# Four fused transformer blocks on one core: batches regrouped from threads of 2, 2, 2, 2 into threads of 1, 2, 2, 2, 1, with other early work and another order of loads

## The chip, the cores and the metric

The kernel runs on one core of a Trainium2 chip, in one launch. The metric is the device time of that launch in microseconds, the lower the better. A core has a matrix engine (PE in the profile, with its weight loads as PEld), a vector engine (DVE), a scalar engine (ACT), a general engine (POOL, GpSimd) and a queue engine (SP) that here only issues DMA transfers. [...]

## The reference

Eight batches of 128 tokens with 256 features (`x`), and a context of the same shape, go through four blocks one after the other, all in float32. The token count and width never change, so what one batch does is independent of the other batches.

```
x = L0(x, ctx)            # attention on ctx, 16 heads of 16 (a0); MLP 256->1024->256 (m0)
x = L1(ctx, x, mask)      # attention on ctx and x together (a1); MLP (m1)
x = L2(x, ctx, ctx)       # two wide attentions on ctx, 16 heads of 128 (l1, l2),
                          # each with a learned extra key and value; MLP (m2)
x = L3(x, ctx, masks)     # self-attention (a4), attention on ctx (a5); MLP (m3)

def _cross_attention(q_in, kv_in, ...):             # the wide attention of L2
    kh = concatenate([(kv_in @ wk + bk), bias_k])   # 16 heads of 128
    vh = concatenate([(kv_in @ wv + bv), bias_v])
    weights = softmax(qh @ kh.T / sqrt(128))
    return (weights @ vh) @ wo + bo
```

Each block adds its result to `x` behind layer norms. The weights are the same for all batches.

## The kernel before, in words

**Threads.** The eight batches are cut into four "threads" of two batches by `SIZES = (2, 2, 2, 2)` (line 25). A thread takes its batches through a0, m0, a1, m1 (its front), then the wide attentions l1 and l2 in four head groups each (its wide part), then m2, a4, a5 and m3 (its back); this is `blocks` (line 1351). A thread loads every weight for itself, with a `loader` (line 505) that holds at most `NW` = 4 of the thread's weight tiles and shares `NWT` = 11 with the others. So each thread moves the full set of weights and bias rows, whatever number of batches it has. Thread h above 1 starts when the front of thread h-2 is done, and above 2 also needs the wide part of thread h-3 to be done.

**The order is planned when the program is built.** The threads are Python generators. A planner (`Plan`, line 83) steps through them with its own estimate of every instruction's duration (`_weight`, line 263) and of the matrix engine's clock (`Clock`, line 226). Whenever an engine is free in that plan, it writes out the most urgent instruction that is ready. The result is a fixed order for each engine. Urgency is a number for each kind of work (`U`, line 64) plus one for each stage of each thread (`LATE`, line 65). When the plan sees the matrix engine idle[...], `idle_work` (line 393) puts in a 128x128 product of the identity matrix whose result nobody reads. I call these fillers; the profile shows them as `mm<-ident`.

**Projections.** `proj` (line 534) multiplies weights, as the stationary operand of 128x128, with the transposed activations of the whole thread: two batches are 256 moving columns. Values, the way back and the scores are made batch by batch, so their shapes do not depend on the thread's size. The front's attentions run one item for each batch (a0) or two (a1), at most two in flight (`flight`, line 445).

**Early wide work.** `AHEAD` (line 63) names head groups whose wide keys and values are computed before the thread's own front, since they need only the context: thread 0 does those of groups 0 and 1 of l1.

**Loads.** All transfers are issued by SP, through `load` and `dma` (lines 408 to 415), in the plan's order, mostly with urgency 0. `value_bias` (line 1282) loads two rows for each wide head group, `bv` and `bb`, spread over 128 partitions, and POOL subtracts them. `bb` has a single buffer; in this version the program takes no slot for it, so the second load of `bb` is issued to SP at once and waits there for the buffer. `inputs` (line 1404) loads `x`, the bias columns `cols` and the context of each thread, and starts it.

Of the kernel before, what the change touches and what calls it, by code (L numbers as in the profile page):

```python
# [15 lines left out]
ALU = mybir.AluOpType  # L16
# [5 lines left out]
NC = D // P  # L22
FF = 4 * D
NF = FF // P
SIZES = (2, 2, 2, 2)
NW, NWT = 4, 11
BIG = 1.0e30

# [31 lines left out]


WARM = True
AHEAD = [[(1, 0), (1, 1)], [], [], []]
U = {'take': 0.33, 'taken': -1, 'norm': 0.36, 'mask': 1.35, 'k': 2.41, 'q': 1.92, 'v': 2.5, 'by key': 0.5, 'softmax': 2.4, 'weights': 0.74, 'pairs': 0.3, 'out': 0.94, 'mlp norm': 0.75, 'mlp 1': 3.6, 'mlp 2': 2.28, 'wide norm': -1, 'wide k': 3.49, 'wide q': 4.0, 'wide v': 4.5, 'wide s': 1.19, 'wide': -0.42, 'ahead': 2.48}
LATE = [(2.3, -0.18, 0.84, -0.88, 1.83, -0.17, 2.53, 1.2, 3.66, 1.59), (7.76, 6.61, 5.49, 5.66, 1.7, 0.2, 4.52, 3.1, 7.31, 7.88), (1.86, 2.79, 2.79, -0.1, 2.14, -1, 4.58, 4.78, 5.62, 1.93), (0.03, 1.63, -0.02, 0.92, 0.05, 2.99, -1, 0.16, -1, -1)]


class Event:
# [14 lines left out]
class Plan:  # L83
# [28 lines left out]
    def spawn(self, gen, urgency, after=0):  # L112
        end = Event()
        self.live[id(gen)] = gen
        self._later(self.now + after, (gen, urgency, end), None)
        return end
# [68 lines left out]
        return start + self.weight  # L185

    def run(self):
        self.now = max(self.until.values())
        while self.events or self.asked:
            while self.events and self.events[0][0] <= self.now:  # L190
                _, _, proc, value = heapq.heappop(self.events)
                self._step(proc, value)
            for eng in self.until:
                if self.until[eng] <= self.now:
                    got = self._choose(eng)
                    if not got and eng == "PE" and self.idle_work and (self.events or self.asked):
                        self.weight = 0
                        if self.clock.lazy(self.now) and self.idle_work():
                            self.until[eng] = self._end(eng)
                            self.log.append((eng, self.now, self.until[eng] - self.now, "idle", 2))  # L200
                    if got:
                        _, a, (_, ns, f, lat, table), load = got
                        self.asked.remove(a)
                        self.weight, self.shared, self.wrote, self.count = ns, False, [], 0
                        if load:
                            self.weight += 1295
                            self.table = table[0]
                        value = f()
                        end = self._end(eng)
                        self.until[eng] = end  # L210
                        self.log.append((eng, self.now, end - self.now, f.__qualname__.replace("four_blocks.<locals>.", "").replace("<locals>.", ""), self.count))
                        self._later(end + (self.SEEN[eng] if lat is None else lat), a[2], value)
            at = [self.events[0][0]] if self.events else []
            at += [t for t in self.until.values() if t > self.now]
            if not at:
                break
            self.now = max(self.now, min(at))
        stuck = []
        for g in self.live.values():
            while g:  # L220
                stuck.append(f"{g.gi_code.co_name}:{g.gi_frame.f_lineno}")
                g = g.gi_yieldfrom
        assert not stuck, f"waits without end: {stuck}"


class Clock:


    W, LITTLE, MUCH = 3413, 0.48, 0.87

    def __init__(self):
        self.t, self.busy, self.fast = 0.0, 0.0, False
# [3 lines left out]
    def lazy(self, now):  # L236

        self._go(now, False)
        self.spans = [(a, b) for a, b in self.spans if b > now - self.W]
        return not self.fast or sum(b - max(a, now - self.W) for a, b in self.spans) < 0.55 * self.W  # L240

    def _go(self, to, busy):
        while self.t < to:
# [19 lines left out]
def _weight(eng, name, args, kw):  # L263

    aps = [x for x in (*args, *kw.values()) if isinstance(x, bass.AP)]
    sizes = [x.free_size() for x in aps]
    n = max(sizes)
    by_part = sum(m == 1 for m in sizes[1:]) if n > 2 else max(0, len(aps) - 2) if name == "tensor_scalar" else 0
    on_sbuf = all(x.space == bass.MemoryType.SB for x in aps)
    if eng == "PE":  # L270
# [9 lines left out]
    if eng == "ACT":  # L280
        if "accum_out" in kw:
            return 385, False
        if name == "copy":
            return 61 + 0.824 * n, False
        return 127 + 0.805 * n + (40 if isinstance(kw.get("bias"), bass.AP) else 0) + (
            90 if isinstance(kw.get("scale"), bass.AP) else 0), False
    if eng == "DVE":
        if name == "reciprocal":
            return 65 + 6.25 * n, False
        if name in ("bn_stats", "bn_aggr"):  # L290
            return (325 if name == "bn_stats" else 99), False
# [47 lines left out]


def op(eng, f, lat=None, table=None):
    return ((eng, 60 if eng == "SP" else 0, f, lat, table),)


EXP = ("exp",)
# [5 lines left out]
def four_blocks(ctx: ExitStack, tc: tile.TileContext, a: dict, out: bass.AP):  # L351
# [36 lines left out]
    row_slots, bv_slots, w_slots = Slots(2), Slots(2), Slots(NWT)  # L388

    def kb():  # L390
        return new(act, [P, 2 * P], "kb", bufs=20)
# [22 lines left out]
    def load(dst, src, kb_):  # L414
        return dma(lambda: nc.sync.dma_start(out=dst, in_=src), kb_)

    ident = new(const, [P, P], "ident")
    make_identity(tc.nc, ident)
# [86 lines left out]
    def loader(T):  # L505
        names = list(weight_list())
        first = {f"l{i}{hg}{x}" for i, hg in AHEAD[T.h] for x in "kv"}
        ahead = [x for x in names if x[0] in first]
        names = [x for x in names if x[0] not in first]
        for name, shape, pieces in names[:2] + ahead + names[2:]:  # L510
            yield (T.w_slots, 1)
            yield (w_slots, 1)
            t = T.w[name] = new(wpool, shape, "w", bufs=NWT)
            ends = [spawn(load(at(t), src, int(np.prod(shape)) // 256 // len(pieces)), 0) for at, src in pieces]
            T.w_in.setdefault(name, Event())
            spawn(all_then(ends, T.w_in[name]), 0)

# [32 lines left out]
    def asks(r):  # L550
        yield r
# [613 lines left out]
    def keys_values(T, i, hg, step_back):  # L1165

        n = f"l{i}{hg}"
        ks, vs = [], []
        bv = new(wpool, [P, 512], "bv", bufs=2)
        bv_in = spawn(value_bias(bv, i, hg), U["mask"] + step_back)  # L1170
        nb, nt = T.nb, T.nt
        v_in = [Event() for _ in range(nb)]

# [22 lines left out]
        def values():  # L1196
# [3 lines left out]
            for b in range(nb):  # L1200
# [9 lines left out]
                        )  # L1210

                def take(p, b=b, t=t):
                    yield op("DVE", lambda: nc.vector.tensor_tensor(t, p, bv, ALU.add))
                    plan.set(v_in[b])
                yield from product([f], take)
            drop(T)
# [74 lines left out]
    def after_scores(T, i, hg, b, s, vs, v_in, n):  # L1291
        t = new(act, [P, 516], "t", bufs=NT_).rearrange("p (h k) -> p h k", h=4)
# [111 lines left out]
    def inputs():  # L1404
        for T in threads:
            h = T.h
            if h == 0:
                first = new(const, [P, 1], "first")
                spawn(asks(op("ACT", lambda: nc.scalar.activation(first, ident[:, :1], AF.Exp), None, EXP)), 0)
            e = spawn(load(T.x, a["x"][T.batches].rearrange("b p d -> p b d"), 128 * T.nb), 0)  # L1410
            spawn(all_then([e], T.ready), 0)
            if h == 0:
                e = spawn(load(cols, a["cols"], 140), 0)
                spawn(all_then([e], cols_in), 0)
            e = spawn(load(T.ctx, a["ctxT"].rearrange("(c p) t -> p c t", p=P)[:, :, T.tokens], 128 * T.nb), 0)
            spawn(all_then([e], ctx_in[h]), 0)
# [48 lines left out]
```

## Time and profile before

| | |
|---|---|
| median of 3 runs | 1214.67 us (1213.44 to 1214.82) |
| the profiled execution | 1218.14 us, of which its span is 1216.3 us |
| mean granted clock of the matrix engine | 0.986 |
| busy: PE, DVE, ACT, POOL | 1163.1, 747.2, 560.3, 340.2 us |
| fillers on PE | 26.5 us in 128 instructions |
| moved by DMA | 145.59 MB, mean 120 GB/s |

Nearly every instruction goes through one helper, so the profile puts it at line 329; groups are told apart by the tiles that they write and read. `mm`, `tl` and `sc` are PSUM tiles: `mm` holds projections and MLP products, `tl` transposes and wide attention products, `sc` the scores of the small attentions. `mm<-hT,w` is a product of normed activations with a weight, `mm<-ctxT,w` one of the context with a weight; `tl<-kb,kb` are the wide scores. One float32 product of full depth stands as two matrix instructions in the trace. The busy time of PE counts a filler as busy[...], so busy is not the same as useful.

### The profile page before, as it was taken

What the parts mean: (1) busy time and instruction counts of PE and PEld (TensorE: products, weight loads), DVE (VectorE), ACT (ScalarE), POOL (GpSimd) and SP (SyncE); (2) the same over time, 40 slices, a digit from 0 to 9 for tenths busy, and PEclk for the clock granted to TensorE, in tenths of its full rate; (3) what the DMA queues carried; (4) which work ended last, traced back from release to release, by engine and by line L of the source; (5) the groups of instructions that cost most, each with busy time, mean ns of one, the idle gap of its engine ahead of it and who ended that gap; (6) DMA issues with size and microseconds to landing.
All of it is one profiled execution on the core that took longest, in us unless ns stands there. A gap on an engine that the chain in (4) does not pass through costs nothing.

```text
span 1216.3 us, 21992 instructions
## 1 busy us (share of the span) xinstructions
PE 1163.1 (96%) x8352; PEld 950.5 (78%) x8352; DVE 747.2 (61%) x1927; ACT 560.3 (46%) x1428; POOL 340.2 (28%) x393
## 2 busy tenths in 40 slices
PE   7998999999999999999999999999999999998988
PEld 6686778888787788887778887887878888876767
DVE  4665846764666384784776725554545475868872
ACT  3345344453443243457365423332424363686962
POOL 3011201122112032044243201121221272566870
PEclk9899998999999999999999999999999999999999
DMA  7623232335325534252532455344454535332120
GB/s 224 198 62 122 71 100 50 105 109 156 104 90 176 172 120 139 89 164 65 150 96 84 126 168 164 102 156 139 148 163 135 150 118 157 107 98 84 38 73 18
DMA packets 107321, 145.59 MB, mean 120 GB/s; under 512 B 6736, under 2 KB 66256, under 8 KB 107216
## 3 DMA queue, kind: packets, MB, share of 16 engines
q1 hardware_dynamic: 107216, 144.18, 38.9%
q8 instruction: 66, 1.08, 0.4%
q14 instruction: 39, 0.32, 0.1%
HBM read 143.11 MB, written 1.05 MB: 119 GB/s over the span
## 4 chain that ended last, share of the span: by engine, by line
PE 74%; DVE 16%; ACT 4%; DMA 3%; issue 1%; POOL 1%; SPq 0%; ACTq 0%; POOLq 0%; DVEq 0%
PE mm L329 54%; PE tl L329 15%; PE sc L329 5%; DVE t L329 2%; DVE tm L329 2%; DVE rz L329 1%; DVE mx L329 1%; DVE mp L329 1%; ACT t L329 1%; DVE q L329 1%; ACT q L329 1%; DVE rv L329 1%; DVE sm L329 1%; POOL t L329 1%; DVE st L329 1%
## 5 line engine op out<-in xcount | busy, mean ns | idle before, releaser
L329 PE MATMUL mm<-hT,w 128*128 128x256 f32 x1216 | 285.7, 383 | 5.5 <-ACT hT L329 1.9
L329 PEld LDWEIGHTS mm<-hT,w 128*128 128x128 f32 x1216 | 224.5, 191 | 42.6 <-ACT kb L329 3.6
L329 POOL TENSOR_TENSOR t<-t,sm 128x512 f32<-128x512 f32 x128 | 131.9, 1042 | 342.7 <-DVE sm L329 265.6
L329 PE MATMUL mm<-ctxT,w 128*128 128x256 f32 x608 | 146.2, 386 | 8.0 <-DVE kb L329 3.6
L329 PE MATMUL mm<-w,ctxT 128*128 128x512 f32 (+1 forms) x352 | 144.6, 542 | 3.9 <-ACT q L329 2.9
L329 POOL TENSOR_TENSOR x<-x,row 128x512 f32<-128x512 f32 x40 | 50.8, 1270 | 318.1 <-ACT xn L329 117.2
L329 PEld LDWEIGHTS mm<-ctxT,w 128*128 128x128 f32 x608 | 112.8, 192 | 25.9 <-issue 4.8
L329 DVE TENSOR_TENSOR x<-mm,x 128x256 f32<-128x256 f32 (+1 forms) x96 | 48.7, 508 | 122.3 <-PE mm L329 121.6
L329 PE MATMUL mm<-w,at 128*128 128x256 f32 x512 | 121.2, 381 | 1.1 <-DVE vw L329 1.1
L329 PE MATMUL mm<-w,kb 128*128 128x256 f32 x512 | 116.5, 380 | 0.0
L329 PEld LDWEIGHTS mm<-w,at 128*128 128x128 f32 x512 | 95.0, 190 | 17.6 <-issue 3.2
L329 PEld LDWEIGHTS mm<-w,kb 128*128 128x128 f32 x512 | 95.8, 190 | 14.6 <-issue 1.3
L329 ACT ACTIVATE t<-t,mn 128x128 f32<-128x128 f32 x256 | 99.0, 393 | 6.0 <-DVE mn L329 5.1
L329 PEld LDWEIGHTS mm<-w,ctxT 128*128 128x128 f32 x352 | 64.5, 193 | 43.5 <-issue 33.1
L329 POOL TENSOR_TENSOR t<-t,mask 128x512 f32<-128x512 f32 x64 | 80.0, 1275 | 13.8 <-DVE t L329 10.8
L329 PE MATMUL tl<-ident,t 128*128 128x128 f32 x512 | 75.6, 277 | 6.2 <-POOL t L329 2.1
L329 ACT ACTIVATE kb<-mm,cols 128x256 f32<-128x256 f32 x128 | 53.0, 472 | 58.9 <-PE mm L329 58.6
L329 PEld LDWEIGHTS tl<-ident,t 128*128 128x128 f32 x512 | 60.0, 142 | 24.6 <-issue 8.9
L329 ACT ACTIVATE kb<-mm,sb 128x256 f32<-128x256 f32 x72 | 32.7, 471 | 91.4 <-PE mm L329 90.6
L329 ACT ACTIVATE at<-tl,cols 128x128 f32<-128x128 f32 x188 | 53.4, 369 | 44.2 <-PE tl L329 44.1
L329 ACT ACTIVATE t<-t 128x516 f32<-128x516 f32 x64 | 40.4, 633 | 72.1 <-DVE t L329 71.9
L329 PEld LDWEIGHTS tl<-kb,kb 128*128 128x128 f32 x512 | 64.3, 192 | 10.3 <-issue 7.7
(118 smaller groups left out, 1800.5 us busy)
## 6 DMA issues: line engine op xcount, KB each, us to landing
w<-in_L_wk SPq DMA_DIRECT2D x32, 512.0 KB, 4.0
w<-in_L_wv SPq DMA_DIRECT2D x32, 512.0 KB, 4.2
w<-in_L_wq SPq DMA_DIRECT2D x32, 512.0 KB, 4.0
w<-in_L_wo SPq DMA_DIRECT2D x32, 512.0 KB, 4.0
bv<-in_L_bv SPq DMA_DIRECT2D x32, 256.0 KB, 4.5
bb<-in_L_bias_v SPq DMA_DIRECT2D x32, 256.0 KB, 5.3
w<-in_L_mlp_w SPq DMA_DIRECT2D x16, 512.0 KB, 4.2
w<-in_L_w_fc SPq DMA_DIRECT2D x16, 512.0 KB, 4.0
```

The source lines that it names most:

```text
L329: return f(*args, **kw)
```

## The change

The batches are cut into five threads of 1, 2, 2, 2 and 1. The early keys and values are those of group 0 of l1 in thread 1, where before they were those of groups 0 and 1 in thread 0. Weight and value-bias loads get an urgency of their own (`U["load"]`), so that the plan may put more urgent loads ahead of them. Inputs of the first two threads, `cols` and thread 0's weights of a0 may also be issued by ACT. The single buffer of `bb` gets a slot (`bb_slots`), so that its load is issued only when the buffer is free, and `bv` is made inside `value_bias` when its slot is there. The planner's figures, the urgencies and the clock thresholds are other numbers. What is computed for each batch is the same.

```
-SIZES = (2, 2, 2, 2)
+SIZES = (1, 2, 2, 2, 1)
-AHEAD = [[(1, 0), (1, 1)], [], [], []]
+AHEAD = [[], [(1, 0)], [], [], []]
-U = {'take': 0.33, ...
+U = {'take': -0.38, ... 'load': -0.79}
...
-        self.now = max(self.until.values())
+        self.until.update({"DVE": 1900, "POOL": 1500, "PE": 1500})
...
-    W, LITTLE, MUCH = 3413, 0.48, 0.87
+    W, LITTLE, MUCH = 3413, 0.41, 0.84
...
-        return not self.fast or sum(...) < 0.55 * self.W
+        return not self.fast or sum(...) < 0.52 * self.W
...
-    return ((eng, 60 if eng == "SP" else 0, f, lat, table),)
+    return ((eng, 480 if eng == "SP" else 0, f, lat, table),)
...
-    def dma(f, kb_):
-
-        yield op("SP", f)
+    def dma(f, kb_, early):
+
+        yield op("SP", lambda: f(nc.sync)) + (op("ACT", lambda: f(nc.scalar)) if early else ())
         plan.dma_until = max(plan.dma_until, plan.now) + kb_ * 2.8
-        yield plan.dma_until - plan.now + 1900
+        yield plan.dma_until - plan.now + 2300
...
-            ends = [spawn(load(at(t), src, ...), 0) for at, src in pieces]
+            early = T.h == 0 and name.startswith("a0")
+            ends = [spawn(load(at(t), src, ..., early), U["load"] - 2 * early)
+                    for at, src in pieces]
...
-        bv = new(wpool, [P, 512], "bv", bufs=2)
-        bv_in = spawn(value_bias(bv, i, hg), U["mask"] + step_back)
+        bv = []
+        bv_in = spawn(value_bias(bv, i, hg, step_back), U["mask"] + step_back)
...
-    def value_bias(bv, i, hg):
+    def value_bias(to, i, hg, step_back):
         s = slice(hg * 512, (hg + 1) * 512)
         yield (bv_slots, 1)
+        bv = new(wpool, [P, 512], "bv", bufs=2)
+        to.append(bv)
+        e = spawn(load(bv, a[f"L2_bv{i}"][:, s].partition_broadcast(P), 256), U["load"] + step_back)
+        yield (bb_slots, 1)
         bb = new(wpool, [P, 512], "bb", bufs=1)
-        e = spawn(load(bv, a[f"L2_bv{i}"][:, s].partition_broadcast(P), 256), 0)
-        yield from load(bb, a[f"L2_bias_v{i}"][:, s].partition_broadcast(P), 256)
+        yield spawn(load(bb, a[f"L2_bias_v{i}"][:, s].partition_broadcast(P), 256), U["load"] + step_back)
         yield e
         yield op("POOL", lambda: nc.gpsimd.tensor_tensor(bv, bv, bb, ALU.subtract))
+        plan.put(bb_slots)
...
     def inputs():
         for T in threads:
             h = T.h
+            early = h < 2
+            rows = (load(T.x, ..., 128 * T.nb, early),
+                    load(T.ctx, ..., 128 * T.nb, early))
+            for f, then in zip(rows, (T.ready, ctx_in[h])):
+                spawn(all_then([spawn(f, -3)], then), 0)
             if h == 0:
+                spawn(all_then([spawn(load(cols, a["cols"], 140, True), -3)], cols_in), 0)
...
-            yield 2000 if h == 0 else 8000
+            yield 4000 if h == 0 else 8000
```

The built program of after holds 481 DMA issues on SP and 5 on ACT, where before had 389 on SP. On PE the shapes that change are these (products of full depth, each two matrix instructions):

| product | before | after |
|---|---|---|
| `mm<-hT,w` and `mm<-ctxT,w`, 256 columns | 912 | 684 |
| the same, 128 columns | 0 | 456 |
| fillers | 64 | 36 |

More of the change, by code (lines that the diff above doesn't have):

```diff
@@ L62 @@
 WARM = True
-AHEAD = [[(1, 0), (1, 1)], [], [], []]
-U = {'take': 0.33, 'taken': -1, 'norm': 0.36, 'mask': 1.35, 'k': 2.41, 'q': 1.92, 'v': 2.5, 'by key': 0.5, 'softmax': 2.4, 'weights': 0.74, 'pairs': 0.3, 'out': 0.94, 'mlp norm': 0.75, 'mlp 1': 3.6, 'mlp 2': 2.28, 'wide norm': -1, 'wide k': 3.49, 'wide q': 4.0, 'wide v': 4.5, 'wide s': 1.19, 'wide': -0.42, 'ahead': 2.48}
-LATE = [(2.3, -0.18, 0.84, -0.88, 1.83, -0.17, 2.53, 1.2, 3.66, 1.59), (7.76, 6.61, 5.49, 5.66, 1.7, 0.2, 4.52, 3.1, 7.31, 7.88), (1.86, 2.79, 2.79, -0.1, 2.14, -1, 4.58, 4.78, 5.62, 1.93), (0.03, 1.63, -0.02, 0.92, 0.05, 2.99, -1, 0.16, -1, -1)]
+AHEAD = [[], [(1, 0)], [], [], []]
+U = {'take': -0.38, 'taken': -1, 'norm': 1.14, 'mask': 4.04, 'k': 2.03, 'q': 0.38, 'v': 2.36, 'by key': 0.44, 'softmax': 1.41, 'weights': 0.4, 'pairs': -0.29, 'out': 1.85, 'mlp norm': 0.59, 'mlp 1': 2.92, 'mlp 2': 3.5, 'wide norm': 1.7, 'wide k': 3.4, 'wide q': 3.15, 'wide v': 4.5, 'wide s': 4.05, 'wide': 0.0, 'ahead': 1.27, 'load': -0.79}
+LATE = [(2.57, -1, -0.28, 0.19, 2.33, 0.01, 3.97, 2.35, 3.3, -0.36), (11.45, 1.43, 1.9, 4.16, -1, -0.96, 3.26, 5.22, 7.47, 5.41), (2.13, 8.62, 4.45, 3.2, 2.52, 0.88, 2.33, 2.26, 2.52, 7.8), (5.21, 8.07, 3.05, 0.78, -0.4, 1.37, 2.54, -0.03, -0.89, 2.66), (1.56, -1, -0.88, 1.22, -0.63, 1.37, 5.13, 1.3, 1.03, 1.13)]
 class Event:
@@ L239, in lazy @@
         self.spans = [(a, b) for a, b in self.spans if b > now - self.W]
-        return not self.fast or sum(b - max(a, now - self.W) for a, b in self.spans) < 0.55 * self.W
+        return not self.fast or sum(b - max(a, now - self.W) for a, b in self.spans) < 0.52 * self.W
     def _go(self, to, busy):
@@ L267, in _weight @@
     n = max(sizes)
+    if name == "dma_start":
+        return 480, False
     by_part = sum(m == 1 for m in sizes[1:]) if n > 2 else max(0, len(aps) - 2) if name == "tensor_scalar" else 0
@@ L284, in _weight @@
             return 61 + 0.824 * n, False
-        return 127 + 0.805 * n + (40 if isinstance(kw.get("bias"), bass.AP) else 0) + (
+        return 127 + 0.805 * n + (35 if on_sbuf and n == 256 else 0) + (40 if isinstance(kw.get("bias"), bass.AP) else 0) + (
             90 if isinstance(kw.get("scale"), bass.AP) else 0), False
     if eng == "DVE":
+        if name == "tensor_scalar" and n == 4 and len(aps) == 2 and len(args) > 5:
+            return 145, False
         if name == "reciprocal":
@@ L290, in _weight @@
         if name in ("bn_stats", "bn_aggr"):
-            return (325 if name == "bn_stats" else 99), False
+            return (330 if name == "bn_stats" else 150), False
         if n <= 8:
@@ L387, in four_blocks @@
     attn_lock, x1_slots = Slots(2), Slots(2)
-    row_slots, bv_slots, w_slots = Slots(2), Slots(2), Slots(NWT)
+    row_slots, bv_slots, bb_slots, w_slots = Slots(2), Slots(2), Slots(1), Slots(NWT)
     def kb():
@@ L406, in col, with load @@
         return cols[:, at : at + n]
-    def dma(f, kb_):
-        yield op("SP", f)
+    def dma(f, kb_, early):
+        yield op("SP", lambda: f(nc.sync)) + (op("ACT", lambda: f(nc.scalar)) if early else ())
         plan.dma_until = max(plan.dma_until, plan.now) + kb_ * 2.8
-        yield plan.dma_until - plan.now + 1900
-    def load(dst, src, kb_):
-        return dma(lambda: nc.sync.dma_start(out=dst, in_=src), kb_)
+        yield plan.dma_until - plan.now + 2300
+    def load(dst, src, kb_, early=False):
+        return dma(lambda eng: eng.dma_start(out=dst, in_=src), kb_, early)
     ident = new(const, [P, P], "ident")
@@ L513, in loader @@
             t = T.w[name] = new(wpool, shape, "w", bufs=NWT)
-            ends = [spawn(load(at(t), src, int(np.prod(shape)) // 256 // len(pieces)), 0) for at, src in pieces]
+            early = T.h == 0 and name.startswith("a0")
+            ends = [spawn(load(at(t), src, int(np.prod(shape)) // 256 // len(pieces), early), U["load"] - 2 * early)
+                    for at, src in pieces]
             T.w_in.setdefault(name, Event())
@@ L1212, in take @@
                 def take(p, b=b, t=t):
-                    yield op("DVE", lambda: nc.vector.tensor_tensor(t, p, bv, ALU.add))
+                    yield op("DVE", lambda: nc.vector.tensor_tensor(t, p, bv[0], ALU.add))
                     plan.set(v_in[b])
@@ L1406, in inputs @@
             h = T.h
+            early = h < 2
+            rows = (load(T.x, a["x"][T.batches].rearrange("b p d -> p b d"), 128 * T.nb, early),
+                    load(T.ctx, a["ctxT"].rearrange("(c p) t -> p c t", p=P)[:, :, T.tokens], 128 * T.nb, early))
+            for f, then in zip(rows, (T.ready, ctx_in[h])):
+                spawn(all_then([spawn(f, -3)], then), 0)
             if h == 0:
+                spawn(all_then([spawn(load(cols, a["cols"], 140, True), -3)], cols_in), 0)
                 first = new(const, [P, 1], "first")
[L1409 to L1416, printed above, removed]
+                spawn(asks(op("ACT", lambda: nc.scalar.activation(first, ident[:, :1], AF.Exp), None, EXP)), 9)
             spawn(blocks(T), 0)
-            yield 2000 if h == 0 else 8000
+            yield 4000 if h == 0 else 8000
     plan.idle_work = idle_work if WARM else None
```

## Prediction

> **What bounds the kernel now.** I read the page first (busy times, slices), then the stages by window, then the shapes of PE's instructions, then the head in order of time.
>
> ```profile
> span 1216.3 us, 21992 instructions
> PE 1163.1 (96%) x8352; PEld 950.5 (78%) x8352; DVE 747.2 (61%) x1927; ACT 560.3 (46%) x1428; POOL 340.2 (28%) x393
> PEclk9899998999999999999999999999999999999999
> ...
> 0.00:200.00 200.00, 180.10 (x1592) 142.39 (x1596) 121.17 (x347) 83.64 (x145) 32.72 (x64) 0.93 0.40 123
> 200.00:550.00 350.00, 344.79 (x2435) 284.90 (x2430) 223.19 (x559) 153.22 (x322) 72.88 (x86) 1.00 0.41 125
> 550.00:650.00 100.00, 93.81 (x717) 74.86 (x716) 67.00 (x165) 57.43 (x173) 40.25 (x45) 0.98 0.37 109
> 650.00:1050.00 400.00, 395.02 (x2353) 325.19 (x2352) 221.18 (x557) 151.95 (x377) 94.58 (x105) 1.00 0.45 138
> 1050.00:1216.30 166.30, 149.38 (x1272) 123.15 (x1270) 114.71 (x302) 114.05 (x416) 99.75 (x95) 0.99 0.22 67
> ```
>
> PE is the bound, but "96% busy" hides slack: it counts fillers, and slow instructions at half clock. So I price PE's work at the full-clock rate of dense bursts. In the next lines a burst ends where the next starts.
>
> ```profile
> 750.90 1.89 PE L329 MATMUL mm<-hT,w 128*128 128x256 f32 x8
> 752.63 1.89 PE L329 MATMUL mm<-ctxT,w 128*128 128x256 f32 x8
> 754.36 0.60 PE L329 MATMUL tl<-ident,t 128*128 128x128 f32 x4
> 754.79 1.06 PE L329 MATMUL tl<-kb,kb 128*128 128x128 f32 x8
> 755.69 1.10 PE L329 MATMUL tl<-pt,vw 128*128 128x128 f32 x8
> 756.63 1.89 PE L329 MATMUL mm<-hT,w 128*128 128x256 f32 x8
> ```
>
> Eight instructions (four products) of 256 columns take 1.73 us (752.63 less 750.90), so a product costs 0.4325 us; eight of 128 columns take 0.90, so 0.224 us a product; a transpose takes 0.109. Likewise from other bursts: 0.86 for a product of 512 columns, 0.069 for a 32-row score of 128 columns (0.1375 for 256), 0.063 for a 32-column value product. Times the counts of the program: 1568 x 0.4325 + 128 x 0.86 + 512 x 0.224 + 736 x 0.109 + 768 x 0.069 + 128 x 0.1375 + 640 x 0.063 = 1094 us. Of the span's 1216.3, 122 us are slack: idle PE, fillers, half clock. Counting the same products inside each window gives the slack by stage: 57 us in 0 to 200 (work 142.6), 12 in 200 to 550, 11 in 550 to 650, 10 in 650 to 1050, 32 from 1050 on. The middle is full; slack sits in the head, where only the fronts of threads 0 and 1 run, and in the tail, where only backs do.
>
> The chain of waits and the timeline show the start of the head:
>
> ```profile
> 2.63 5.35 DMA bv<-in_L_bv
> 8.00 8.35 DMA row<-in_rows
> ...
> 16.52 1.27 POOL x L329
> 17.79 1.23 POOL bv L329
> ...
> 19.41 4.72 DMA mask<-in_mask_b
> ...
> 3.62 0.43 SPq L415 DMA_DIRECT2D w<-in_L_k_w  x1
> 10.32 9.05 SPq L415 DMA_DIRECT2D bb<-in_L_bias_v  x2
> 19.89 0.43 SPq L415 DMA_DIRECT2D x<-in_x  x1
> 11.21 3.54 PE L329 MATMUL mm<-ctxT,w 128*128 128x256 f32 x8 [1.29 <-DMA w<-in_L_k_w]
> ```
>
> The first projection waits until 11.21 for a weight issued at 3.62, behind two value biases. Then SP stands 9 us on the second `bb`, whose single buffer POOL frees at about 19, and all of thread 1's inputs stand behind it.
>
> **The change, part by part.**
>
> *Smaller threads on PE.* 228 products of 256 columns (98.6 us) become 456 of 128 (102.1): +3.5 us, all on PE. `tl<-kb,kb` is the near row: full depth, a new stationary operand for each product, 128 columns. [...] The trace's float32 burst pays 1.80 for 1.73, so I take +3.5[...].
>
> *Head.* Thread 0 with one batch has half the elements and half the attention items in each front step. By PE's order in the built program its first wide scores come after 99.6 us of work, where before had 139.6; from there wide work of thread 0 fills the waits of the fronts of threads 1 and 2. In the order of before, 48 of 64 fillers stand ahead of that point (21.2 us busy in 0 to 200), in after 27. Scaled so, 57 us of slack become 57 x 27/48 = 32: -25. As the clock thresholds for fillers changed too, I check by the other end: the same slack share on less work, 99.6 x 57/142.6 = 40, less the 5 us by which the first weight comes sooner, so -22. Against it stands that only one early group (6.9 us of keys and values) is left to fill the first waits, two (13.8) before. I take -22; the ends are -8 (only the load gains below) and -35.
>
> *Loads.* In after SP's first issues are the context, the key weight and the query weight of thread 0, while ACT issues `x`, `cols` and two more weights; the biases come 16th and 17th. At 0.45 us each, the key weight is issued by 1.7. About 0.7 to 0.9 MB are then ahead of or beside it, 3 to 5 us at 170 to 240 GB/s, plus 2: lands at 5 to 7 where 11.2 was. Thread 1's mask is SP's ninth issue; with 3 MB ahead at 240 GB/s it lands at 14 to 16, where 24.1 was. This is inside the -22, and is its part for which nothing else has to hold. The five issues cost ACT 2.3 us in front of its table load and `xn`; before, ACT idles 6.00 us there, so nothing. POOL's subtraction moves with `bb`; nobody but the early values waits for it.
>
> *Tail.* Behind the last wide exponential in ACT's order stand 160 exponentials before (61.8 + 30.7 us of ACT with their sums), 128 in after: -18.5 us of ACT, where ACT is 69% busy. But that stretch holds 17 table loads for 9, +10 us. Work left on PE behind the last wide product grows from 124 to 135 us, so denser. Fillers fall from 16 to 7. I take -7 of the 32; ends -15 and +3.
>
> *More table loads.* The order holds 69 table loads, 42 before. The trace:
>
> ```profile
> 71.10 1.88 ACT L329 ACTIVATE pt<-sc 128x2048 f32<-128x2048 f32 x1 [0.63 <-PE sc L329]
> 72.99 1.28 ACT L329 ACT_TABLE_LOAD   x1
> 74.29 1.57 ACT L329 ACTIVATE kb<-mm,cols 128x256 f32<-128x256 f32 x4
> ```
>
> Neither side shows a gap, so 27 x 1.28 = 35 us of ACT. [...]it is hidden where ACT idles 54%, and not where a front's chain runs through it. With some 190 more small DVE instructions (0.17 us each, 33 us on an engine idle 39%) I put +3 on the path, between 0 and +12.
>
> *A fifth pass of weights.* +35 MB, one thread's share of 145.6, so 181 MB, 151 GB/s on average; slices of before reach 224. In 200 to 1050 PE waits for DMA 1.4 us in all. SP's 92 further issues are covered as long as a slot is freed a landing (4.0 us) ahead: +1, between 0 and +25.
>
> Sum: +3.5 -22 -7 +3 +1 = -21.5. Span 1216.3 -> 1194.8; the profiled execution took 1218.14, so 1196.6; the median of the runs is 3.5 below that execution, so about 1193.
>
> **The rivals.**
>
> *The plan is right only on paper (small gain).* The order is fixed at the build. If PE waits in order for results that the plan thought sooner, head fillers go but idle time stays. Only the loads' -8, +3.5 and -3 in the tail are left, -7 or so: 1207. For it: already in before the longest head waits are not those that fillers cover. Against: two of the listed waits are SP's own and vanish by construction.
>
> *A fuller head and tail.* Ends of -35 and -12 with +6: 1174.
>
> *Slower: the single DMA queue.* Threads 0 and 4 have 16 wide groups of one batch, each needing 2 MB of weights for 10.8 us of PE instead of 21.6. SP issues in a fixed order and stands on PE in before already (824 us in all). If the load of one such group stands behind a slot of another thread, PE idles up to a landing, 4 us, in each stage of it. It decides at 21.5/16 = 1.35 us of uncovered wait a group; at 2.5 us it is 1193 + 40 = 1233. Against: two larger threads are nearly always there to fill in, 5 MB for 33 us is 155 GB/s.
>
> That the change isn't made can be left out: the built order has the 128-column products and ACT's five issues.
>
> **How the numbers follow.** The sum's case, 1180 to 1203: 0.62. Small gain, 1203 to 1212: 0.17. Fuller, under 1180: 0.09. No change: 0.04. Slower: 0.08. The median's runs lie within 0.1%, so a measurement can tell about 0.2%, 2.4 us. Range 1176 to 1213, which leaves out most of the slower case and the far end of the fuller one.
>
> **What would show it.** Right: first `mm<-ctxT,w` at 5 to 7 us, no SP issue of 9 us, thread 1's mask by 16; first `tl<-kb,kb` scores of the wide part near 135 us instead of 197; fillers under 15 us busy; the 128-column `mm` bursts at 0.9 us for eight; PE's waits for DMA under 5 us in all. Wrong: those bursts over 1.1 us, PE waiting for `w` from DMA in the stretch of one-batch groups, or a head as slack as before.

## The result: 6 us faster, a quarter of what was predicted

| | before | after |
|---|---|---|
| median | 1213.36 us (8 runs, 1210.47 to 1217.82) | 1207.38 us (8 runs, 1204.73 to 1211.73) |
| ratio to before | | 0.9950, 95% interval 0.9930 to 0.9969 |
| the profiled execution, its span, its mean clock | 1218.14, 1216.3, 0.986 | 1206.24, 1204.5, 0.996 |

The prediction said 1193. In two further sets of runs the ratio of after was 0.9946 (0.9925 to 0.9967) and 0.9973 (0.9959 to 0.9988). Part of the gain comes with a higher granted clock: its median is 0.991 over the 95 runs of before that stand beside the experiments, and 0.994 over the 31 runs of after. Where the clock is the same, the kernels are closer: at 0.993 the medians are 1210.3 us (6 runs) and 1209.0 (8 runs), at 0.994 they are 1209.8 (8 runs) and 1206.8 (7 runs). So half of the 6 us or more goes with the clock. Whether the changed order raised it by leaving PE fewer gaps is not shown.

The page of after, its lines of span, busy time and granted clock:

```profile
span 1204.5 us, 23333 instructions
PE 1153.0 (96%) x8752; PEld 953.6 (79%) x8752; DVE 787.5 (65%) x2120; ACT 610.3 (51%) x1534; POOL 358.4 (30%) x437
PEclk8999999999999999999999999999999999999999
```

Its stages by window (columns as before: busy PE, PEld, DVE, ACT, POOL, then granted clock, DMA share, GB/s):

```profile
0.00:200.00 200.00, 179.02 (x1734) 147.39 (x1735) 143.14 (x412) 93.86 (x180) 37.78 (x71) 0.97 0.55 171
200.00:550.00 350.00, 342.62 (x2451) 283.72 (x2450) 222.81 (x601) 165.50 (x377) 89.30 (x116) 1.00 0.49 151
550.00:650.00 100.00, 97.73 (x870) 80.42 (x869) 64.41 (x176) 50.98 (x90) 14.23 (x24) 1.00 0.42 133
650.00:1050.00 400.00, 394.31 (x2544) 327.28 (x2543) 252.12 (x646) 189.27 (x522) 132.41 (x141) 1.00 0.53 164
1050.00:1204.50 154.50, 139.36 (x1160) 114.81 (x1158) 104.98 (x287) 110.72 (x367) 84.64 (x85) 1.00 0.30 94
```

PE is busy 96% of the span in both kernels, so busy time says nothing about the change; DMA runs at 133 to 171 GB/s up to 1050 us, where it ran at 109 to 138, and PE's list of waits holds none for a transfer. So I count as the prediction did: the products inside a stretch times the dense rates are its work, and the stretch less its work is slack. I cut at the first wide scores (`tl<-kb,kb`), since the head ends there. The other kernels of the table are the experiments below.

| one profiled execution of | work | head ends at | slack in the head | slack behind |
|---|---|---|---|---|
| before | 1094.1 | 197.2 | 57.5 | 64.8 |
| `b_no_stall` | 1094.1 | 189.4 | 49.8 | 61.8 |
| `b_early` | 1094.1 | 187.8 | 48.1 | 61.2 |
| `b_halves` | 1097.6 | 193.4 | 53.2 | 64.6 |
| `b_split` | 1097.6 | 135.9 | 44.2 | 157.2 |
| after | 1097.6 | 139.8 | 40.2 | 66.7 |
| `a_mask_first` | 1097.6 | 135.9 | 36.3 | 67.8 |
| `a_big_late` | 1097.6 | 133.1 | 33.5 | 67.7 |
| `a_big_again`, the same kernel | 1097.6 | 137.5 | 38.0 | 67.4 |

The last two rows tell how much one profile can be off: 4.5 us in the head, with a mean clock of 1.00 in the first execution and 0.996 in the second. From before to after the work grows by 3.5, the head's slack falls by 17.3 and the slack behind grows by 1.9: 11.9 us between the two profiled executions. The medians are only 6.0 apart, because the profiled execution of before lay 4.8 above its median and that of after 1.1 below.

What the head's 17.3 are made of is read from the sums of two windows that end where the head ends (the first number is the width). First before, then after:

```profile
sum 197.00, PE 177.10 PEld 139.73 DVE 119.21 ACT 82.08 POOL 32.72; mean PE 29.52 PEld 23.29 DVE 19.87 ACT 13.68 POOL 5.45
```

```profile
0.00:10.00 10.00, 6.30 (x30) 6.11 (x30) 4.18 (x29) 1.57 (x3) 5.09 (x20) 1.00 0.70 230
10.00:20.00 10.00, 8.31 (x52) 6.55 (x53) 6.27 (x23) 3.08 (x7) 0.73 (x1) 0.52 0.96 306
...
sum 140.00, PE 120.05 PEld 97.59 DVE 96.71 ACT 62.62 POOL 29.32; mean PE 24.01 PEld 19.52 DVE 19.34 ACT 12.52 POOL 5.86
```

PE idles 19.9 us in both heads (197.00 - 177.10, and 140.00 - 120.05). What fell is fillers, 20.7 to 9.7 us on PE, and time in which instructions took longer than their dense rate, 16.8 to 10.5; that is in part clock, whose mean in the head is 0.93 in before's profile and 0.96 in after's: the eight instructions of 128x256 at 11.21 in before took 3.54 us at a granted clock of 0.55, those of the dense burst at 750.90 took 1.89 at 1.00. And the first 20 us became worse, 15.6 us of slack where before had 12.6: PE does 4.4 us of work in them, and from 10 to 20 us its granted clock is 0.52.

The timeline shows why (`SPq` and `ACTq` are DMA issues on those queues; columns: start, duration, engine, instruction, and what ended the idle time before it):

```profile
2.24 0.52 ACTq L333 DMA_DIRECT2D w<-in_L_cproj_w  x1
2.79 1.28 ACT L333 ACT_TABLE_LOAD   x1 [2.79 <-issue]
3.67 0.88 SPq L420 DMA_DIRECT2D w<-in_L_fc_w  x2
3.68 0.43 DVE L333 BATCH_NORM_STATS2 st<-x 128x6 f32<-128x256 f32 x1 [0.93 <-DMA x<-in_x]
6.21 1.44 PE L333 MATMUL mm<-ctxT,w 128*128 128x128 f32 x8
9.43 0.37 ACTq L333 DMA_DIRECT2D x<-in_x  x1
9.43 0.23 DVE L333 TENSOR_SCALAR mask<-mask 128x128 f32<-128x128 uint8 x1 [3.06 <-DMA mask<-in_mask_b]
9.91 0.60 ACT L333 ACTIVATE xn<-x,rz,ry 128x256 f32<-128x256 f32 x1 [5.62 <-DMA w<-in_L_fc_w]
10.57 0.69 PE L333 MATMUL tl<-ident,xn 128*128 128x128 f32 x2 [2.92 <-ACT xn L333]
16.16 2.43 PE L333 MATMUL sc<-k,q 32*128 32x128 f32 x32 [0.61 <-ACT q L333]
```

The first projection starts at 6.21, as predicted. Then PE has nothing until 10.57. Thread 0's `xn` is ready to run at 6.4, when DVE has its factors, but in ACT's order thread 1's `x` stands ahead of it, the fifth transfer that ACT issues. ACT's first four issues followed one another from 0.73 to 2.76, with 0.03 us between them; this one began at 9.43, when thread 0's mask had landed and DVE took it up. On SP the fifth issue, `fc_w`, stood too: it began at 3.67, after a wait of 1.0 us that SP's list of waits puts down to the landing of `x`. So I take it that ACT's issue stood for the landing of the mask. That is my estimate, from the two starts at 9.43; the profile puts ACT's idle time down to `fc_w`, and why an issue stands for an earlier transfer is not shown. ACT idled 5.6 us ahead of `xn`; DVE stood for the same mask.

### The profile page after: what moved, and what is told of

It reads as the page before. It is cut to its first block, busy times and chain, and to the rows that moved or that the text cites. A ratio compares the mean times of both kernels' runs of the same rounds, so it can differ in the third digit from the quotient of the medians.

```text
span 1204.5 us, 23333 instructions
## 1 busy us (share of the span) xinstructions
PE 1153.0 (96%) x8752; PEld 953.6 (79%) x8752; DVE 787.5 (65%) x2120; ACT 610.3 (51%) x1534; POOL 358.4 (30%) x437
## 4 chain that ended last, share of the span: by engine, by line
PE 70%; DVE 17%; ACT 7%; POOL 2%; issue 2%; DMA 1%; ACTq 0%; POOLq 0%; DVEq 0%
PE mm L333 51%; PE tl L333 16%; PE sc L333 4%; DVE rz L333 3%; ACT t L333 2%; POOL t L333 2%; DVE t L333 2%; DVE mp L333 1%; ACT L333 1%; ACT kb L333 1%; DVE mn L333 1%; DVE ry L333 1%; DVE st L333 1%; ACT pt L333 1%; DVE q L333 1%
## 5 line engine op out<-in xcount | busy, mean ns | idle before, releaser
L333 PE MATMUL mm<-hT,w 128*128 128x256 f32 (+1 forms) x1520 | 296.2, 342 | 15.4 <-DVE kb L333 3.0
L333 PEld LDWEIGHTS mm<-hT,w 128*128 128x128 f32 x1520 | 242.7, 191 | 53.2 <-ACT kb L333 5.8
L333 PE MATMUL mm<-ctxT,w 128*128 128x256 f32 (+1 forms) x760 | 149.3, 341 | 2.9 <-DVE x L333 1.6
L333 PEld LDWEIGHTS mm<-ctxT,w 128*128 128x128 f32 x760 | 121.9, 192 | 18.7 <-issue 2.3
L333 POOL TENSOR_TENSOR x<-x,row 128x512 f32<-128x512 f32 (+1 forms) x50 | 52.6, 1052 | 198.7 <-ACT xn L333 106.7
L333 POOL TENSOR_TENSOR bv<-bv,bb 128x512 f32<-128x512 f32 x40 | 50.8, 1269 | 160.4 <-DMA bb<-in_L_bias_v 138.6
L333 ACT ACTIVATE kb<-mm,cols 128x256 f32<-128x256 f32 (+1 forms) x160 | 59.8, 429 | 45.4 <-PE mm L333 44.8
L333 ACT ACTIVATE kb<-mm,sb 128x256 f32<-128x256 f32 (+1 forms) x90 | 36.4, 426 | 87.1 <-PE mm L333 85.5
```

Source lines behind the costliest of these rows:

```text
L333: return f(*args, **kw)
```

## The experiments

Each was timed beside runs of the kernel before on the same chip; a ratio is to those. The first four ran together (before: 1213.08), then `b_no_stall`, `b_halves`, `a_mask_first` and `b_split` (1213.56), then `a_pair`, `a_big_late`, `a_cold` and `b_cold` (1211.32), then `b_early` and `a_big_again` (1211.42).

**`a_again` and `a_pair`: after, unchanged.**

> The changed kernel once more, as the base for the runs beside it and for how far two profiles of one kernel differ. Expected: 1207 us, ratio 0.995 to before, granted clock 0.991 to 0.996. If the first profile stood for all, its slack by stage comes back within 2 us: 40 in the head (to the first wide scores near 140 us), 67 behind it.

> The kernel after once more, as the measure for the three that run beside it: 1206.5 to 1208 by both theories.

1207.16 (9 runs, ratio 0.9946) and 1207.85 (14 runs, ratio 0.9973). The gain is 3.5 to 6 us.

**`a_x1_on_sp`: ACT no longer stands.** Thread 1's `x` is issued by SP in the place where ACT issued it.

```
-            rows = (load(T.x, ..., 128 * T.nb, early),
+            rows = (load(T.x, ..., 128 * T.nb, early, h == 1),
...
+        f(nc.sync if on_sp else nc.scalar)
```

> The changed kernel with one edit: thread 1's x is issued by SP instead of ACT, at the same place of the program; the order on every engine is the same otherwise. Theory 1 (ACT's fifth DMA issue[...] holds thread 0's xn behind it): xn starts at 6.4 us instead of 9.91, the first query product about 3 us sooner than 13.48, and the time falls by 2 to 3.5 us. Rival (the time is set by later waits that stand at fixed places, so what is won at the start is lost again at the next wait): xn is as early, but the time stays within 1 us of the changed kernel.

1206.99 (7 runs, ratio 0.9942, 0.9921 to 0.9963): nothing that can be told from `a_again`, so the rival holds. Its timeline:

```profile
6.48 0.60 ACT L333 ACTIVATE xn<-x,rz,ry 128x256 f32<-128x256 f32 x1 [2.19 <-DVE rz L333]
7.14 0.44 PE L333 MATMUL tl<-ident,xn 128*128 128x128 f32 x2 [0.24 <-ACT xn L333]
9.71 0.23 DVE L333 TENSOR_SCALAR mask<-mask 128x128 f32<-128x128 uint8 x1 [3.26 <-DMA mask<-in_mask_b]
15.25 2.43 PE L333 MATMUL sc<-k,q 32*128 32x128 f32 x32 [0.61 <-ACT q L333]
```

`xn` comes 3.4 us sooner and the first scores 0.9: DVE still stands for the mask until 9.71, with the copy of `hT` behind it. PE stands for the value weight in the same way: it waits 2.04 us for that transfer, until 9.61. One of several waits with about the same end was taken away.

**`a_mask_first`: DVE no longer stands either.** As above, and thread 0's mask (16 KB) is SP's first issue instead of its fourth.

```
+        if name == "mask_b" and T.h == 0:
+            first.append(lambda eng: eng.dma_start(out=raw, in_=src))   # issued ahead of SP's first
```

> The kernel after with thread 1's x on SP's queue (as in a_x1_on_sp) and thread 0's first mask as SP's first issue instead of its fourth; nothing else moves. Thread 0's xn then starts at 6.5 us and its mask is on the chip by 4 to 5, so neither holds DVE; the first scores sc<-k,q come at 13 to 14 us, where they came at 16.2 in after and 15.3 in a_x1_on_sp. Theory that the first 20 us set the head: 2 to 3 us less than after. Rival (what comes sooner waits later, as a_x1_on_sp suggests, or is eaten by fillers and the clock): within 1 us of after, 1206.5 to 1207.5.

1204.45 (6 runs, ratio 0.9919, 0.9899 to 0.9940). In the timeline the mask is used at 7.36, and the scores start 2.4 us sooner than in after:

```profile
7.36 0.22 DVE L333 TENSOR_SCALAR mask<-mask 128x128 f32<-128x128 uint8 x1
7.66 2.05 PE L333 MATMUL mm<-ctxT,w 128*128 128x128 f32 x8 [1.24 <-DMA w<-in_L_k_w]
13.77 0.50 PE L333 MATMUL sc<-k,q 32*128 32x128 f32 x8 [0.61 <-ACT q L333]
```

Head slack 36.3, time 2.7 us under `a_again`: the first theory holds. But the key weight now lands later, so the bytes ahead of it may be the next limit.

**`a_big_late`, run again as `a_big_again`: bytes that nobody waits for go last.** As above, and `cproj_w` and the two `fc_w` of thread 0 stand behind thread 1's inputs.

```
-SP:  mask ctxT k_w q_w fc_w fc_w row x1 ctxT1 mask1 k_w1 ...      ACT: x cols v_w cproj_w
+SP:  mask ctxT k_w q_w row x1 ctxT1 mask1 k_w1 cproj_w fc_w fc_w ...   ACT: x cols v_w
```

> As a_mask_first, and three weights of thread 0 that are used last (cproj_w and both fc_w, 1.25 MB together) are issued behind thread 1's x, context, mask and key weight instead of ahead of them. Theory (the first 12 us wait for bytes: in a_mask_first v_w, k_w and x land 1 to 2 us later than x and k_w did in after): the first mm<-ctxT,w at 5 to 6.5 us (7.7 in a_mask_first), first scores at 12 to 13, and 1 to 1.5 us less than a_mask_first, so 1203. Rival (from there DVE and ACT, not bytes, set the pace): first scores at 13.5 or later, time within 1 us of a_mask_first's 1204.5; if the three weights then come late for thread 0's product with cproj_w and its MLP, slower.

> a_big_late once more, beside b_early on one chip: 1201.5 to 1203.5. By theory A of b_early the two lie within 5 us of each other, by B 7 us or more apart.

1202.44 (6 runs, ratio 0.9927, 0.9906 to 0.9948) and 1203.68 (6 runs, ratio 0.9927, 0.9903 to 0.9951). On the same chip `a_pair` took 1207.85, so the order of loads in the head is worth about 5 us on the kernel after, part of it again with a higher clock (medians 0.994 and 0.997). By its ratio to before it is no faster than `a_mask_first` (0.9919), so a gain of this last step is not shown. Timeline and windows:

```profile
6.60 1.13 PE L333 MATMUL mm<-ctxT,w 128*128 128x128 f32 x8 [0.94 <-DMA w<-in_L_k_w]
7.39 0.60 ACT L333 ACTIVATE xn<-x,rz,ry 128x256 f32<-128x256 f32 x1 [3.72 <-DVE rz L333]
8.04 0.44 PE L333 MATMUL tl<-ident,xn 128*128 128x128 f32 x2 [0.32 <-ACT xn L333]
11.89 0.50 PE L333 MATMUL sc<-k,q 32*128 32x128 f32 x8 [0.61 <-ACT q L333]
```

```profile
0.00:10.00 10.00, 6.74 (x36) 5.93 (x36) 6.33 (x42) 3.55 (x7) 5.71 (x21) 1.00 0.74 226
10.00:20.00 10.00, 8.87 (x100) 7.37 (x101) 8.47 (x28) 2.25 (x6) 0.00 (x0) 1.00 1.04 360
```

The scores start 4.3 us sooner than in after, and the clock from 10 to 20 us is 1.00 instead of 0.52: the empty 3 us from 7.6 went with half speed for what followed them. In another profile of after, `a_again`, PE stands 4.45 us at this place; its clock is 0.81 over the first 20 us, where it is 0.76 in after and 1.00 in `a_big_late`.

**`a_no_switch` and `b_no_switch`: what do table loads cost?** The MLPs' gelu becomes the identity function, so that nearly all table loads go (68 of 69 in after, 41 of 42 in before).

```
-     hs[i][:, : T.nt], p[...], func, bias=col(b1, m + i)), None, table)
+     hs[i][:, : T.nt], p[...], AF.Identity, bias=col(b1, m + i)), None, table)
```

> The changed kernel with the identity in place of the gelu functions, which leaves the gelus out; the order on all engines is the same, but 68 of 69 table loads of ACT are gone (87 us of ACT). Theory 2 (the 27 table loads more are on the path: the chain of waits holds 14.1 us of table loads in after, 1.3 in before): it falls by 10 us or more, and by at least 5 us more than the same edit saves on the kernel before. Rival (ACT has room): both kernels fall alike, by less than 5 us.

> The kernel before with the identity in place of the gelu functions, which leaves the gelus out; same order, 41 of 42 table loads gone (52 us of ACT). Theory 2: it falls by little, 1 to 5 us, since 1.3 us of its chain are table loads. Rival: as much as the changed kernel does with the same edit.

1204.03 (6 runs, ratio 0.9926, 0.9901 to 0.9951) and 1209.88 (22 runs, ratio 0.9970, 0.9957 to 0.9983): 3.1 us under `a_again` and 3.2 under before. Both fall alike, so the 27 additional loads are not where the gain went; a cost of much more than 3 us for them is unlikely, a smaller one is not excluded. The stretches behind the cut fall by 3.7 and 6.0 us of slack, the heads by nothing beyond their spread.

**`b_no_stall`: before without the wait of SP.** The second `bb` is not loaded and POOL subtracts `bv` from itself. PE, DVE and ACT keep their order.

```
-        yield from load(bb, a[f"L2_bias_v{i}"][:, s].partition_broadcast(P), 256)
+        yield from dma(lambda: None if second else nc.sync.dma_start(out=bb, ...), 256)
```

> The kernel before without its second load of bb (POOL then subtracts bv from itself, so one bias of the wide values comes out as zero); the order of PE, DVE and ACT is the same, and SP no longer stands 9.05 us, so that thread 1's inputs are issued about 9 us sooner. Theory of the prediction (the loads alone are worth some 8 us of the head, part of it this stall): 3 to 8 us less than before, and the head's slack up to the first tl<-kb,kb falls from 57 to 50 or under. Rival (the head is held by the chain of thread 0's front, and thread 1's inputs are not late for PE): within 1.5 us of before, with a head slack of 55 to 58.

1208.12 (6 runs, ratio 0.9944, 0.9924 to 0.9964): 5.4 us from one wait of a queue, nearly all of what the whole change brought. The head's slack is 49.8. Behind the one `bb` that is left, thread 1's `x` is issued at 10.95 instead of 19.89:

```profile
9.45 0.34 SPq L1291 DMA_DIRECT2D bb<-in_L_bias_v  x1
10.22 0.33 SPq L415 DMA_DIRECT2D mask<-in_mask_b  x1
10.95 0.38 SPq L415 DMA_DIRECT2D x<-in_x  x1
```

**`b_early`: before with its loads in order of need.** Every engine's order is kept; on SP the two `bv` go behind the query weight, and the second `bb` (complete here) behind thread 1's mask, `x`, context and four weights.

```
-SP:  mask x cols ctxT bv bv k_w v_w q_w cproj_w wk wv row bb bb mask1 x1 ctxT1 k_w1 ...
+SP:  mask x cols ctxT k_w v_w q_w bv bv cproj_w wk wv row bb mask1 x1 ctxT1 k_w1 v_w1 q_w1 cproj_w1 bb ...
```

> The kernel before, all engines' orders kept, only SP's loads of the head reordered: the two loads of bv behind the query weight instead of ahead of the key weight, and the second bb (complete here, other than in b_no_stall) behind thread 1's mask, x, context and four weights instead of ahead of them. Theory A (the loads alone carry about what the whole change gained; the split's head gain is given back by the smaller products and behind): the key weight lands 2 to 3 us sooner, thread 1's inputs are issued by 13 us, and the time is 5 to 8 us under before, no slower than after. Theory B (the split carries it): at most 3 us under before.

1204.98 (6 runs, ratio 0.9943, 0.9925 to 0.9962), 6.4 us under before, with threads of 2, 2, 2, 2 and the old plan. SP's part of the timeline: thread 1's `x` is issued at 10.84 instead of 19.89, and up to and with the second `bb` no issue stands for more than 2.2 us.

```profile
2.63 0.47 SPq L424 DMA_DIRECT2D w<-in_L_k_w  x1
...
9.54 0.33 SPq L424 DMA_DIRECT2D mask<-in_mask_b  x1
10.84 0.38 SPq L424 DMA_DIRECT2D x<-in_x  x1
...
18.03 0.34 SPq L429 DMA_DIRECT2D bb<-in_L_bias_v  x1
```

`a_big_again` beside it is 1.3 us faster, with runs from 1200.06 to 1206.70 against 1202.55 to 1206.96. So with the loads of both kernels in order, the split with its plan is worth 1.3 us, which these runs cannot tell from nothing: theory A holds.

**`b_halves`: the price of smaller products.** In before, every fourth group of 256 columns is issued as two of 128, as many as after has, in the same order.

```
+                for part in (slice(0, P), slice(P, 2 * P)):
+                    for to, k in plan.held:
+                        f(to[:, part], **{**k, "rhs": k["rhs"][:, part]})
```

> The kernel before with every fourth accumulation group of 256 columns (hT,w and ctxT,w) issued as two of 128 columns: 228 products of 256 become 456 of 128, as many as in after, in an order that is else the same. Theory of the prediction (0.224 us for 128 columns, 0.4325 for 256): +3.5 us. Rival, from the trace of after (an instruction of 128 columns takes 0.118 us on average behind the first wide scores, one of 256 0.221, so a product 0.236 and 0.442): 456 x 0.236 - 228 x 0.442 = +6.8 us. Third (hidden in waits[...]): 0[...].

1219.00 (21 runs, ratio 1.0050, 1.0035 to 1.0065): 5.4 us slower, 4.2 to 7.9. Its bursts run at the rate that I had taken, 0.90 us for eight:

```profile
702.80 1.05 PE L336 MATMUL mm<-hT,w 128*128 128x128 f32 x8
703.70 2.76 PE L340 MATMUL mm<-hT,w 128*128 128x256 f32 x12
```

So the rate stands, but +3.5 lies below the measured interval and the rival's +6.8 inside it. The runs' clock was lower too (median 0.989, against 0.990 in the runs of before beside them), which may be a part: where the clock is the same, the difference to before is 3.6 us at 0.991 (4 runs against 26) and 6.2 at 0.987 (4 against 7). These runs do not decide between the two.

**`b_split`: before with threads of 1, 2, 2, 2 and 1, and nothing else.**

```
-SIZES = (2, 2, 2, 2)
+SIZES = (1, 2, 2, 2, 1)
```

> The kernel before with threads of 1, 2, 2, 2 and 1 batches and nothing else of the change: biases, loads and queues as before, thread 0 with two early groups, the same weights of its planner (the fifth thread has the fourth's due times). Its first wide scores stand behind 91.7 us of work (99.6 in after, 139.6 before). Theory (the split makes the head's gain: the share of slack stays, on less work): the head's slack is 0.41 x 92 = 38 to 42 us, and the head ends at 128 to 136; what the untuned order loses behind it is not the change's. Rival (loads make it): the slack stays over 48. The whole: unclear, 1200 to 1230, as this order holds 100 fillers in the tail.

1301.19 (5 runs, ratio 1.0716). Its head ends at 135.9, as the theory says, with a slack of 44.2, between the 38 to 42 of the theory and the rival's 48. The whole was expected at 1200 to 1230 and is far outside: behind the head it loses 90 us more than after, since due times made for four threads let the fifth run alone at the end. So this edit doesn't give the price of the split; that would need due times of its own.

**`a_cold` and `b_cold`: no fillers.** `WARM` is off; the orders are planned again.

```
-WARM = True
+WARM = False
```

> The kernel after without its fillers (WARM off; the order is planned again and differs a little). Its trace has 12 us of fillers on PE in the head up to the first wide scores. Theory (a filler stands in a wait and costs nothing, and keeps the clock up): without them those 12 us turn into idle time and the clock falls, 3 to 12 us slower than after. Rival (fillers cost their own time[...]): 2 to 6 us faster.

> The same on the kernel before, which has 48 fillers in the head (20.7 us on PE there) and 16 in the tail. Theory (the head's gain of the change, 11 us of fillers and 6 us of slow clock, is time in which PE had nothing to do, filled or not): 5 to 20 us slower than before, and the difference between the two kernels without fillers is at least as large as with them (6 us or more). Rival (the gain is that the change drops fillers that cost time): without fillers the two kernels come within 3 us of each other, apart from the +3.5 to +5.4 of the smaller products.

1211.67 (14 runs, ratio 1.0001), 3.8 us over `a_pair`, at a median clock of 0.990 against 0.994; and 1239.04 (5 runs, ratio 1.0237), at 0.979 against 0.991 in the runs of before beside it. The head of `b_cold` has 57.6 us of slack, as before has with 48 fillers (57.5); that of `a_cold` 41.4, within after's 38 to 41. So in the head fillers stand in waits and cost next to nothing, and the 11 us of fillers that the change takes away are waits that it takes away. As both orders were planned anew, this holds for the sums, not for each wait. The 28 us of `b_cold`, where 5 to 20 were expected, lie elsewhere: the slack behind the point where 134 us of work are left is 52.6, before's 32.3. That is another plan of the tail, and I draw nothing from it.

## Why the prediction was wrong, step by step

Direction, range and the signs in the trace were right: the first projection at 6.21 us, no issue of 9 us on SP, thread 1's mask on the chip at 15.0, first wide scores at 139.8 (135 was said), fillers 12.3 us on `mm`, 128-column bursts of eight at 0.89, no waits of PE for transfers. The size was wrong by 15.5 us (-21.5 said, -6.0 measured). Three terms of the sum were wrong, with about equal weight.

- **The reference, 5.9.** "The median of the runs is 3.5 below that execution" was carried over to after as a constant. It isn't: the profiled execution of before was a run with a low clock, and part of its 57 us of slack was that. Over the 95 runs of before the median is 1215.2 at a mean clock of 0.988 (11 runs), 1212.3 at 0.991 (26) and 1209.8 at 0.994 (8); the profile had 0.986. The slack to be won should have been priced at the usual clock. The three runs that "lie within 0.1%" understated the spread too: eight runs of before reach from 1210.47 to 1217.82.
- **Head, -17.3 instead of -22: 4.7.** The second route said "the same slack share on less work": 40 us, and after has 40.2. That this fits so well is in part luck: `b_split` has 44.2 on less work still (91.7), and after's 40.2 holds a wait that two of the experiments remove. What failed is "less the 5 us by which the first weight comes sooner". The weight came sooner; thread 0's `xn` and mask did not. I had written that "the five issues cost ACT 2.3 us" in idle time, "so nothing"; but the fifth stood for 5 us with `xn` behind it. I had priced how long an issue takes, not what it waits for. With that mended, in `a_mask_first` and `a_big_late`, the head's slack is 33.5 to 38.0, and about the missing 5 us are there.
- **Behind the first wide scores, +1.9 instead of -3: 4.9.** The tail alone did gain, 3.4 us behind the point where 134 us of work are left (32.3 to 28.9), half of the -7. It is given back ahead of it. Behind the first wide scores PE changes from one kind of instruction to another (other tiles or another shape) 653 times in before and 791 times in after, and what instructions take beyond their dense rate lies almost all at these changes, 24.2 us and 30.7, 0.037 and 0.039 each. Why it grows is not shown. The number of changes alone is not the cause: `b_halves` has some 110 more of them there than before, by cutting bursts in two, and its slack behind the head is 64.6 us, where before has 64.8. The next fence shows one burst of eight that costs 0.89 us and one that costs 1.00 (each up to the next start); my rates came from dense bursts alone.

```profile
117.81 1.05 PE L333 MATMUL mm<-ctxT,w 128*128 128x128 f32 x8
118.70 0.38 PE L333 MATMUL tl<-ident,mp 128*128 128x128 f32 x2
...
1018.69 1.16 PE L333 MATMUL mm<-hT,w 128*128 128x128 f32 x8
1019.69 0.49 PE L333 MATMUL tl<-ident,t 128*128 128x128 f32 x3
```

Of the other terms, the table loads (+3) are not seen as a difference between the kernels, where they could have been up to 3; the fifth pass of weights (+1) shows no wait of PE; the +3.5 for smaller products is right as a rate, but 5.4 us (4.2 to 7.9) were measured for it in `b_halves`.

The deeper error is in the weights of the causes. I took the loads for 8 us of the 22 and the split for the rest. `b_early` has the loads alone and is as fast as after: 6.4 us. From `b_early` to the mean of the two profiles of `a_big_late`, the split's own account is -12.3 in the head (48.1 to 35.8), +3.5 work and +6.3 behind (61.2 to 67.5): -2.5. The +6.3 is more than the +1.9 above because before's profile had a lower clock behind its head too, 0.996 against 1.00, an estimate of 4 us in 1019. So the rival that I gave 0.17, "the plan is right only on paper", was right in its number (1207) and close in its sum: the loads' -8, +3.5 and -3 in the tail. Its reason holds in part: idle time did stay at 19.9 us, but the fillers that went were waits too, and what the head won by them was paid back behind it.

What stays open is how the 6.0 us of the change itself divide between its loads and its split, since no run has after with the loads of before; `b_early` shows that loads alone can give as much, not that they did. Open too is how much of the 6.3 behind belongs to the split as such and how much to this particular plan of it, since every other division of the batches would need due times of its own, and how much of each gain comes only by way of the clock.

## What to carry to other kernels

Ahead of costing a regrouping, put the first transfers in order of need and look at each queue for an issue that waits: here that alone gave what a new division of the work with a new plan gave. A transfer issued from a compute engine's queue is priced by what its issue can wait for (5.1 us here, on ACT from 4.29 to 9.43), and by what stands behind it there. And gains that are read as slack from one profile must be set against the usual clock of many runs, and against what shorter bursts lose everywhere else (5.4 us in `b_halves`).

## What the runs showed of the hardware

- A transfer's issue could stand for an earlier transfer: in after SP's fifth, `fc_w`, began at 3.67, after 1.0 us that the profile puts down to the landing of `x`. ACT's fifth, thread 1's `x`, began at 9.43, as DVE took up the mask that had just landed; ACT had done nothing since 4.29.
- What stood behind such an issue stood with it: thread 0's `xn`, ready at 6.4, ran at 9.91 on ACT, and at 6.48 when SP issued that transfer (`a_x1_on_sp`). On SP thread 1's `x` was issued at 19.89 behind 9.05 us of issuing `bb`, and at 10.95 with the second `bb` left out (`b_no_stall`).
- After 2.9 us without work on PE, its granted clock was 0.52 for the ten microseconds from 10 to 20 in after; in `a_big_late`, where the gap was closed, 1.00.
- In before, eight matrix instructions of 128x256 took 3.54 us at a granted clock of 0.55 and 1.89 at 1.00.
- Runs of one kernel differed with their mean clock: before took 1215.2 us at 0.988 and 1209.8 at 0.994.
- Taking away 68 table loads of 1.28 us each (87 us of ACT) brought 3.1 us on after, and taking away 41 brought 3.2 on before.
- At changes from one kind of matrix instruction to another PE took 0.04 us more than the dense rate on average, 24.2 us in the profile of before (653 changes) and 30.7 in that of after (791).
